# Every second band of two 3x3 convolutions formed from four mixtures of input rows (24 passes instead of 36)

## The chip, the cores and the metric

The kernel runs on one core of a Trainium2 chip. The metric is the time of one execution in microseconds (us). A core has five engines that run side by side, each with its own queue worked off in order: TensorE (PE in the profile; PEld is its loading of weights), VectorE (DVE), ScalarE (ACT), GpSimd (POOL) and SyncE (SP, which here only issues transfers). TensorE writes its sums to PSUM, a memory of 8 banks of 512 fp32 values per partition; everything else works on SBUF.

## What is computed

The input x is 4 images of 128 channels and 64 x 64 points, fp32. Two layers follow each other; cut to what matters:

```python
# layer 0: attention over the 4096 points of an image, 4 heads of 32 channels
x = x + proj(softmax(q @ k.T / sqrt(32)) @ v)      # q, k, v from the group-normed x
# layer 1: two convolutions with weights quantised to the integers -4..3 times alpha
def conv3x3(x, wq):                                # zero border of one point
    out = 0
    for kh in range(3):
        for kw in range(3):
            out = out + einsum('bchw,oc->bohw', xp[:, :, kh:kh+H, kw:kw+W], wq[:, :, kh, kw])
    return out
out = relu(batchnorm(conv3x3(x, wq1)))             # mean and variance over all images and points
out = relu(batchnorm(conv3x3(out, wq2)) + x)
```

A batch norm needs all results of its convolution before it can scale any of them.

## The kernel before, in words

**Attention first.** Most of the kernel is the attention (lines 425 to 769): scores (L442) and their weighting of v (L456) on TensorE, exponentials on ScalarE (L444), sums of exponentials on VectorE (L471). Its result y0 goes to DRAM, image by image. During its last blocks the first bands of the first convolution are already loaded and split.

**A band.** The convolutions work on 16 bands (`bandlist`), each 16 rows of one image (`BR`), 4 bands an image. A band's input tile has 18 rows of 66 points: the rows above and below and the border columns, which GpSimd sets to zero (`border`). TensorE multiplies here in a rounded form of fp32 (`F32R`). So the input is split (`split`): `hi` is the rounded input, a cast on VectorE (L573), and `lo` the rest, a subtraction (L574). `conv` makes one half of a band, 8 rows or 512 points, in one PSUM bank: for `hi` and then `lo`, nine taps each, a matmul (here "pass") of 512 columns against the 128 x 128 weights of that tap: 18 passes a half, 36 a band (L782). The weights are small integers, exact in the rounded form.

**A layer.** `layer(i, prepare, done)` goes through the bands. For each it queues the passes of the band; calls `prepare(m)`; then for each half queues statistics on VectorE (L848, read from PSUM) and a copy of the results to `cv` on ScalarE (L849). All queues keep this order: what `prepare(m)` gives to VectorE and ScalarE stands ahead of the statistics and copies of band m. Bands 0 and 1 of layer 0 are made before `layer` starts (`early`), between the last steps of the attention. The last band's halves have tiles of their own, and its statistics are merged with the others' at the end (L850 to L858). Then follow some idle matmuls (`keep_warm`) and `batch_norm`, which gives the scale and shift that the next stage needs.

**What prepare does.** In layer 0 it is `first(m)`: it issues the load of band m+3 (SP's queue) and splits band m+2. At m = 2 it loads the quantised weights of the second convolution from DRAM to `raw_w`, at m = 6 it casts them to `wq[1]`, at m = 5 `count_bad` counts values out of bounds, with a tiny matmul and a copy of its result on VectorE. In layer 1 it is `second(m)`: `relu_band` of band m+2 (a relu on ScalarE from `cv`, L891, then cast and subtraction on VectorE, L894 and L895), and the load of a part of y0 for the residual. The first input of layer 1 is made apart, in two pieces (L906 to L918).

**Buffers.** The input tiles `t`, `hi`, `lo` come from a pool of 9 (`kpool`, through `stack_tile`); a tile's place is used again when everything that read it is done. PSUM is `pss`, three tiles of two banks, one per ordinary band (`conv_tile`), and `psa`, two tiles of one bank, for the last band and small sums. The framework places all waits; on a PSUM tile, the operations of different engines are kept in the order in which they are written.

**The end.** After layer 1 the results are scaled, the residual is added (L948), the relu applied (L949) and the output stored.

Of the kernel before, what the change touches and what calls it, by code (L numbers as in the profile page):

```python
# [16 lines left out]
F32 = mybir.dt.float32  # L17
AF = mybir.ActivationFunctionType
ALU = mybir.AluOpType
# [3 lines left out]
P = 128  # L23
# [3 lines left out]
TAPS = 9  # L27
FB = 512
# [6 lines left out]
F32R = mybir.dt.float32r  # L35
# [43 lines left out]
def _fast_body(ctx, tc, x, norm_w, norm_b, qkv_wt, qkv_b, proj_wt, proj_b,  # L79
               w1, alpha1, gamma1, beta1, w2, alpha2, gamma2, beta2, out, cnt):  # L80
    nc = tc.nc
    B, C, H, W = x.shape
# [3 lines left out]
    NB = N // FB  # L86
# [3 lines left out]
    PW = W + 2  # L90
# [48 lines left out]
    wq = [const.tile([P, TAPS, P], F32R, name="wq0")]  # L139
    wqd = dram.tile([P, TAPS, P], F32, name="wqd")  # L140
# [68 lines left out]
    pss = ctx.enter_context(tc.tile_pool(name="pss", bufs=3, space=PSUM))  # L209
    psa = ctx.enter_context(tc.tile_pool(name="psa", bufs=2, space=PSUM))  # L210
    y0 = [dram.tile([P, N], F32, name=f"y0_{b}") for b in range(B)]
    BR = 2 * RB
# [11 lines left out]
    def stack_tile(name):  # L224
        return kpool.tile([P, KW], F32R, name=name, tag="k")

    def f32(t):
        return t.bitcast(F32)
# [326 lines left out]
    def band_tile(name):  # L555
        return stack_tile(name).rearrange("p (r w) -> p r w", w=PW)

    def border(t, g):

        nc.gpsimd.memset(f32(t)[:, :, 0:1], 0.0)  # L560
        nc.gpsimd.memset(f32(t)[:, :, W + 1 : W + 2], 0.0)
        r0, r1 = g * BR - 1, g * BR + BR + 1
        if r0 < 0:
            nc.gpsimd.memset(f32(t)[:, 0, 1 : 1 + W], 0.0)
        if r1 > H:
            nc.gpsimd.memset(f32(t)[:, BR + 1, 1 : 1 + W], 0.0)
        lo, hi = max(r0, 0), min(r1, H)
        return f32(t)[:, lo - r0 : hi - r0, 1 : 1 + W], lo, hi

    def split(t, name):  # L570

        hi, lo = band_tile(f"hi{name}"), band_tile(f"lo{name}")
        nc.vector.tensor_copy(hi, f32(t))  # L573
        nc.vector.tensor_tensor(lo, f32(t), f32(hi), ALU.subtract)  # L574
        return hi, lo

    raw, ready = {}, {}

    def load_band(b, g):
        raw[b, g] = t = band_tile(f"t0_{b}_{g}")  # L580
        inner, lo, hi = border(t, g)
        nc.sync.dma_start(out=inner, in_=y0[b].rearrange("p (h w) -> p h w", w=W)[:, lo:hi, :])

    def split_band(b, g):
        ready[0, b, g] = split(raw[b, g], f"0_{b}_{g}")


    halves = [ppool.tile([P, HEADS, FB], F32, name=f"xh{i}", tag="p") for i in range(2)]
# [6 lines left out]
    st = small.tile([P, NB, 6], F32, name="st0", tag="st")  # L595
# [144 lines left out]
    todo, parts = [], {}  # L740
# [29 lines left out]

    bandlist = [(b, g) for b in range(B) for g in range(H // BR)]

    def conv(parts, ps, j, w):
        hi, lo = parts
        r0 = j * RB
        n = 0
        for part in (hi, lo):
            for tap in range(TAPS):  # L780
                kh, kw = divmod(tap, 3)
                nc.tensor.matmul(ps.rearrange("p (r w) -> p r w", w=W), w[:, tap, :],  # L782
                                 part[:, r0 + kh : r0 + kh + RB, kw : kw + W],
                                 start=(n == 0), stop=(n == 2 * TAPS - 1))
                n += 1

    def conv_tile(i, b, g):
        return pss.tile([P, 2, FB], F32, name=f"c{i}_{b}_{g}", tag="s")
# [16 lines left out]

    mid = ctx.enter_context(tc.tile_pool(name="mid", bufs=1))
    cv = [mid.tile([P, N], F32, name=f"cv{b}") for b in range(B)]
    raw_w = mid.tile([P, TAPS, P], F32, name="raw_w")
    wq.append(mid.tile([P, TAPS, P], F32R, name="wq1"))


    a_q, a_g, a_n = ([small.tile([P, 1], F32, name=f"{n}{i}") for i in range(2)]
# [21 lines left out]
    def layer(i, prepare, done):  # L834


        st = mid.tile([P, B * NB, 6], F32, name=f"st{i}")
        end = mid.tile([P, 15], F32, name=f"end{i}")
        nc.gpsimd.memset(end[:, 0:1], float((B * NB - 2) * FB))
        for m, (b, g) in enumerate(bandlist[:-1]):  # L840
            ps = done[m] if m < len(done) else conv_tile(i, b, g)
            for j in range(2):
                if m >= len(done):
                    conv(ready[i, b, g], ps[:, j, :], j, wq[i])
            prepare(m)
            for j in range(2):
                c = 2 * g + j
                nc.vector.bn_stats(st[:, b * NB + c, :], ps[:, j, :])  # L848
                nc.scalar.copy(cv[b][:, c * FB : (c + 1) * FB], ps[:, j, :])  # L849
        nc.vector.bn_aggr(end[:, 1:3], st.rearrange("p j s -> p (j s)")[:, : 6 * B * NB - 12])  # L850
        nc.vector.tensor_scalar(end[:, 2:3], end[:, 2:3], float((B * NB - 2) * FB), None, ALU.mult)
        b, g = bandlist[-1]
        for j in range(2):
            ps = psa.tile([P, FB], F32, name=f"c{i}_last{j}", tag="a")
            conv(ready[i, b, g], ps, j, wq[i])
            c = 2 * g + j
            nc.vector.bn_stats(end[:, 3 + 6 * j : 9 + 6 * j], ps)
            nc.scalar.copy(cv[b][:, c * FB : (c + 1) * FB], ps)  # L858
        prepare(len(bandlist) - 1)
        keep_warm(10)  # L860
        return batch_norm(i, end)

    def count_bad():

        big = small.tile([P, 1], F32, name="big")
        nc.vector.tensor_reduce(big, worst, AX.X, ALU.max)
        bad = small.tile([P, 1], F32, name="bad")
        nc.vector.tensor_scalar(bad, big, LIMIT, None, ALU.is_gt)
        nbad = psa.tile([P, FB], F32, name="nbad", tag="a")
        nc.tensor.matmul(nbad[0:1, 0:1], bad, ones[:, 0:1], start=True, stop=True)  # L870
        nc.vector.tensor_copy(cnt, nbad[0:1, 0:1])

    def first(m):
        if m == 5:
            count_bad()
        if m == 2:
            nc.sync.dma_start(out=raw_w, in_=wqd)
        if m == 6:
            nc.vector.tensor_copy(wq[1], raw_w)
        if 0 < m < len(bandlist) - 3:  # L880
            load_band(*bandlist[m + 3])
        if m + 2 < len(bandlist) and m > 0:
            split_band(*bandlist[m + 2])

    a1, c1 = layer(0, first, early)

    def relu_rows(b, g, t, r0, r1):
# [8 lines left out]
                                f32(t["hi"])[:, r0:r1, :], ALU.subtract)  # L896

    def relu_band(b, g, pieces=((0, BR + 2),)):
        t = {n: band_tile(f"{n}1_{b}_{g}") for n in ("t", "hi", "lo")}
        t["inner"] = border(t["t"], g)  # L900
        for r0, r1 in pieces:
            relu_rows(b, g, t, r0, r1)
        ready[1, b, g] = t["hi"], t["lo"]


    b0, g0 = bandlist[0]  # L906
    t = {n: band_tile(f"{n}1_{b0}_{g0}") for n in ("t", "hi", "lo")}
    t["inner"] = border(t["t"], g0)
    hi_inner, lo_row, hi_row = border(t["hi"], g0)
    for r0, r1 in ((0, RB + 2), (RB + 2, BR + 2)):  # L910
        a, e = max(r0 + g0 * BR - 1, lo_row), min(r1 + g0 * BR - 1, hi_row)
        for dst in (hi_inner.bitcast(F32R), t["inner"][0]):
            nc.scalar.activation(dst[:, a - lo_row : e - lo_row, :],
                                 cv[b0].rearrange("p (h w) -> p h w", w=W)[:, a:e, :], AF.Relu,
                                 bias=c1, scale=a1)
# [26 lines left out]
    for b in range(B):  # L942
        for j in range(4):
            for p in range(2 if b == j == 0 else 1):
                n = HN // 2 if b == j == 0 else HN
                y = res[b, j][:, p * n : (p + 1) * n]
# [464 lines left out]
```

## Time and profile before

| what | us |
|---|---|
| median of 3 runs | 2547.48 (2546.02 to 2547.59) |
| the profiled execution | 2548.74 |
| its span, first to last instruction | 2547.0 |
| TensorE busy (share of the span) | 2509.0 (99%) |
| VectorE busy | 2137.2 (84%) |
| ScalarE busy | 2087.4 (82%) |
| passes of the convolutions, L782, one on average | 0.400 to 0.401 (pipelined: the next starts earlier) |
| first pass of layer 0 (band 0) starts at | 2234.0 |
| last statistics of layer 0 start at | 2375.32 |
| first pass of layer 1 starts at | 2378.84 |
| last statistics of layer 1 start at | 2516.48 |

Times inside the profile are counted from the first instruction of the span. A row of the groups gives line, engine, operation, output and inputs by the program's names, partitions x elements, how many, their busy time, the mean of one in ns, and the idle time of the engine just before them with what ended it. In the answers in order of time a row is one or several like instructions: start, length, engine, line; in brackets the idle time before it and what ended that. Matmuls overlap, so the cost of one is read from the distance of the starts, not from its length.

### The profile page before, as it was taken

The numbers are of one execution on the slowest core, as the hardware profiler recorded it, in microseconds if no ns is written. First come the engines' busy times: TensorE is split into PE (matmuls) and PEld (weight loads), VectorE is DVE, ScalarE is ACT, GpSimd is POOL, SyncE is SP. The second block draws the span as 40 slices with busy tenths as digits, with TensorE's granted clock in tenths as the row PEclk, the third lists the DMA queues.
The fourth block names the chain that finished last, engine by engine and source line by source line (L and its number), as shares of the span: only waits on it lengthen the run. The fifth ranks groups of instructions, "written<-read, shape, count | busy, mean of one in ns | idle before, by whom it ended". The sixth has DMA issues, their size and how long they took to land.

```text
span 2547.0 us, 65043 instructions
## 1 busy us (share of the span) xinstructions
PE 2509.0 (99%) x28708; PEld 1503.6 (59%) x28708; DVE 2137.2 (84%) x1402; ACT 2087.4 (82%) x2278; POOL 281.6 (11%) x461
## 2 busy tenths in 40 slices
PE   9999999999999999999999999999999999999995
PEld 6555555555555555555555555555555555577774
DVE  6899888889988889889988888889999999954445
ACT  5999888999988999999988899989999999911224
POOL 2111111111011111110111111111000011000000
PEclk9999999999999999999999999999999999999998
DMA  6877667788757667797766666796666666745004
GB/s 193 192 185 169 168 173 181 171 203 182 184 132 190 170 152 169 164 231 164 173 163 172 157 166 158 191 203 150 149 138 144 146 145 149 150 90 160 1 1 166
DMA packets 148954, 403.86 MB, mean 159 GB/s; under 512 B 59416, under 2 KB 60184, under 8 KB 120120
## 3 DMA queue, kind: packets, MB, share of 16 engines
q0 software_dynamic: 45840, 280.39, 48.2%
q1 hardware_dynamic: 100952, 113.60, 16.9%
q10 hardware_dynamic: 1872, 5.64, 0.6%
q8 instruction: 227, 3.72, 0.6%
q14 instruction: 63, 0.52, 0.1%
HBM read 107.48 MB, written 56.42 MB: 64 GB/s over the span
## 4 chain that ended last, share of the span: by engine, by line
PE 92%; issue 3%; DMA 2%; DVE 1%; ACT 1%; ACTq 0%; POOL 0%; SPq 0%; POOLq 0%; DVEq 0%
PE s L442 41%; PE acc L456 36%; PE c L782 9%; DMA rm<-p 2%; PE l L488 1%; PE pq L317 1%; PE pk L317 1%; PE po L317 1%; PE pv L317 1%; DVE r L471 1%; ACT p L444 0%; ACT res L949 0%; DMA xh<-in_x_dram 0%; PE c_last L782 0%; DVE res L948 0%
## 5 line engine op out<-in xcount | busy, mean ns | idle before, releaser
L444 ACT ACTIVATE p<-s 128x1024 f32<-128x1024 f32 x2048 | 1950.5, 1032 | 201.6 <-PE s L442 154.5
L471 DVE TENSOR_TENSOR r<-r,p 128x2048 f32<-128x2048 f32 x768 | 1758.2, 2289 | 65.0 <-ACT p L444 14.5
L442 PE MATMUL s<-q,k 64*128 64x512 f32 x8192 | 1138.6, 409 | 1.7 <-ACT p L444 0.9
L456 PE MATMUL acc<-p,v 128*32 128x256 f32 x16384 | 1026.4, 383 | 0.0
L442 PEld LDWEIGHTS s<-q,k 64*128 64x128 f32 x8192 | 715.4, 184 | 410.3 <-issue 165.3
L456 PEld LDWEIGHTS acc<-p,v 128*32 128x32 f32 x16384 | 462.4, 109 | 483.7 <-issue 248.5
L466 POOL DMA_DIRECT2D rm<-p x160 | 139.5, 872 | 800.4 <-ACT p L444 535.5
L849 ACT COPY cv<-c 128x512 f32<-128x512 f32 x60 | 35.2, 586 | 200.1 <-DVE st L848 200.1
L782 PE MATMUL c<-hi,wq 128*128 128x512 f32 x540 | 139.1, 401 | 1.3 <-issue 1.3
L782 PE MATMUL c<-lo,wq 128*128 128x512 f32 x540 | 138.5, 400 | 0.0
L848 DVE BATCH_NORM_STATS2 st<-c 128x6 f32<-128x512 f32 x60 | 41.9, 699 | 103.9 <-PE c L782 83.4
L782 PEld LDWEIGHTS c<-hi,wq 128*128 128x128 f32 x540 | 101.2, 188 | 30.3 <-issue 2.1
L782 PEld LDWEIGHTS c<-lo,wq 128*128 128x128 f32 x540 | 101.6, 188 | 27.2
L352 DVE SCALAR_TENSOR_TENSOR kst<-pk,b,kst 128x512 fp32r<-128x512 f32 x32 | 24.0, 751 | 83.6 <-PE s L442 68.5
L469 DVE TENSOR_TENSOR r<-p,p 128x2048 f32<-128x2048 f32 x32 | 73.2, 2288 | 12.1 <-ACT p L444 11.1
L352 DVE SCALAR_TENSOR_TENSOR qst<-pq,b,qst 128x512 fp32r<-128x512 f32 x32 | 24.0, 751 | 58.2 <-PE s L442 47.3
L356 POOL DMA_DIRECT2D qd<-qst x31 | 23.6, 760 | 262.7 <-DVE qst L352 220.8
L492 POOL DMA_DIRECT2D r<-rm x31 | 26.2, 844 | 220.4 <-DMA rm<-p 95.1
L356 POOL DMA_DIRECT2D kd<-kst x27 | 20.0, 740 | 175.8 <-DVE kst L352 167.2
L488 PE MATMUL l<-r,ones 128*32 128x256 f32 (+1 forms) x504 | 37.7, 382 | 0.0
L464 POOL DMA_DIRECT2D rm<-p x32 | 17.8, 557 | 176.8 <-ACT p L444 93.4
L351 ACT ACTIVATE kst<-pk,b 128x512 fp32r<-128x512 f32 x32 | 22.3, 699 | 18.2 <-PE pk L317 18.2
(149 smaller groups left out, 739.3 us busy)
## 6 DMA issues: line engine op xcount, KB each, us to landing
rm<-p POOLq DMA_DIRECT2D x192, 1024.0 KB, 7.9
q<-qd SPq DMA_DIRECT2D x248, 128.0 KB
r<-rm POOLq DMA_DIRECT2D x31, 1024.0 KB, 7.6
x<-in_x_dram SPq DMA_DIRECT2D x86, 256.0 KB
k<-kd SPq DMA_DIRECT2D x124, 128.0 KB
qd<-qst POOLq DMA_DIRECT2D x31, 512.0 KB, 5.3
kd<-kst POOLq DMA_DIRECT2D x27, 512.0 KB, 4.8
y<-x POOLq DMA_DIRECT2D x32, 256.0 KB, 6.2
```

Source lines behind the costliest of these rows:

```text
L317: nc.tensor.matmul(out[cs, :], w[:, cs], x, start=True, stop=True)
L352: nc.vector.scalar_tensor_tensor(lo, ps[what], bias, t[:, 0, :], ALU.add, ALU.subtract)
L356: (nc.sync if start else nc.gpsimd).dma_start(out=dst[b, j].rearrange("s p n -> p s n"), in_=t)
L442: nc.tensor.matmul(s[:, i, :], k[r, half, c0 : c0 + P], q[r, half, part, :], start=(part == 0), stop=(part == 1))
L444: nc.scalar.activation(pts[step][:, 2 * half : 2 * half + 2, :], s, AF.Exp, scale=SCALE)
L456: nc.tensor.matmul(acc[n][h * D : (h + 1) * D, cs], v[:, kt % KB, h * D : (h + 1) * D], pt[:, h, cs], start=(kt == 0 and half == 0), stop= ...
L466: nc.gpsimd.dma_start(out=msum[n], in_=pt, accum_op=ALU.add)
L469: nc.vector.tensor_tensor(rsum[n], pts[step - 1], pt, ALU.add)
L471: nc.vector.tensor_tensor(rsum[n], rsum[n], pt, ALU.add)
L488: nc.tensor.matmul(t["l"][h * D : (h + 1) * D, cs], ones, r[:, h, cs], start=first, stop=end)
L782: nc.tensor.matmul(ps.rearrange("p (r w) -> p r w", w=W), w[:, tap, :], part[:, r0 + kh : r0 + kh + RB, kw : kw + W], start=(n == 0), stop ...
L848: nc.vector.bn_stats(st[:, b * NB + c, :], ps[:, j, :])
```

## The change

With rows d0 to d3 of the input and the three rows of weights g0, g1, g2, two neighbouring rows of results are

- m0 = (d0 - d2) g0, m1 = (d1 + d2) (g0 + g1 + g2)/2, m2 = (d2 - d1) (g0 - g1 + g2)/2, m3 = (d1 - d3) g2
- upper row: m0 + m1 + m2; lower row: m1 - m2 - m3

Each product is a convolution along the row alone, with 3 taps. For the 16 rows of a band each product has 8 rows, 512 points: 3 taps for `hi` and 3 for `lo`, 6 passes, and four products, 24 passes. Bands 3, 5, 7, 9, 11, 13 of layer 0 and 2, 4, 6, 8, 10, 12, 14 of layer 1 (`BY_TWO`) are made in this way; the others as before.

- `mixed` takes the place of `split` there: on VectorE the differences (`outer`, 16 rows) and the two halves of `inner` (8 rows each), on ScalarE the two rounded copies, on VectorE the two rests. Three of its tiles come from `kpool` (as does the input), three from a new pool of 6 (`upper`).
- `mix_weights` makes (g0+g1+g2)/2 and (g0-g1+g2)/2 on VectorE, for layer 0 ahead of the layer, for layer 1 at band 14.
- `conv_by_two` forms m1 and m2 in a tile of `pss`, then m0 and m3 in a second tile of `pss` or, every second time, in the two tiles of `psa`.
- `rows_of_two` combines them: a copy on ScalarE and four operations on VectorE, straight into `cv`. The statistics then read `cv` in SBUF; the two copies to `cv` fall away.
- The weights of the second convolution are loaded to a tile of `kpool` at band 5 instead of to `raw_w` at band 2; `count_bad` comes at band 4 instead of 5.

```diff
--- before.py
+++ after.py
@@ -575,6 +575,35 @@
         return hi, lo
 
     raw, ready = {}, {}
+    bandlist = [(b, g) for b in range(B) for g in range(H // BR)]
+
+
+
+
+    BY_TWO = (set((3, 5, 7, 9, 11, 13)), set((2, 4, 6, 8, 10, 12, 14)))
+
+    def mixed(t, name):
+
+
+        t = f32(t)
+        outer, inner = (stack_tile(f"{n}{name}")[:, : BR * PW].rearrange("p (r w) -> p r w", w=PW)
+                        for n in ("vo", "vi"))
+        nc.vector.tensor_tensor(f32(outer), t[:, 0:BR, :], t[:, 2 : BR + 2, :], ALU.subtract)
+        odd, even = t[:, 1 : BR + 1 : 2, :], t[:, 2 : BR + 2 : 2, :]
+        nc.vector.tensor_tensor(f32(inner)[:, : BR // 2, :], odd, even, ALU.add)
+        nc.vector.tensor_tensor(f32(inner)[:, BR // 2 :, :], even, odd, ALU.subtract)
+        def part(n):
+            if n == "uo":
+                return stack_tile(f"{n}{name}")[:, : BR * PW].rearrange("p (r w) -> p r w", w=PW)
+            return upper.tile([P, BR, PW], F32R, name=f"{n}{name}", tag="u")
+
+        hi, lo = ([part(n + k) for k in "oi"] for n in "ul")
+        for u, v in zip(hi, (outer, inner)):
+            nc.scalar.copy(u, f32(v))
+        for u, v, w in zip(hi, (outer, inner), lo):
+            nc.vector.tensor_tensor(w, f32(v), f32(u), ALU.subtract)
+        return [(o[:, 0::2, :], i[:, : BR // 2, :], i[:, BR // 2 :, :], o[:, 1::2, :])
+                for o, i in (hi, lo)]
 
     def load_band(b, g):
         raw[b, g] = t = band_tile(f"t0_{b}_{g}")
@@ -582,7 +611,8 @@
         nc.sync.dma_start(out=inner, in_=y0[b].rearrange("p (h w) -> p h w", w=W)[:, lo:hi, :])
 
     def split_band(b, g):
-        ready[0, b, g] = split(raw[b, g], f"0_{b}_{g}")
+        way = mixed if bandlist.index((b, g)) in BY_TWO[0] else split
+        ready[0, b, g] = way(raw[b, g], f"0_{b}_{g}")
 
 
     halves = [ppool.tile([P, HEADS, FB], F32, name=f"xh{i}", tag="p") for i in range(2)]
@@ -770,8 +800,6 @@
 
 
 
-    bandlist = [(b, g) for b in range(B) for g in range(H // BR)]
-
     def conv(parts, ps, j, w):
         hi, lo = parts
         r0 = j * RB
@@ -805,8 +833,41 @@
 
     mid = ctx.enter_context(tc.tile_pool(name="mid", bufs=1))
     cv = [mid.tile([P, N], F32, name=f"cv{b}") for b in range(B)]
-    raw_w = mid.tile([P, TAPS, P], F32, name="raw_w")
     wq.append(mid.tile([P, TAPS, P], F32R, name="wq1"))
+    upper = ctx.enter_context(tc.tile_pool(name="upper", bufs=6))
+    wmix = mid.tile([P, 2, 3, P], F32R, name="wmix")
+
+    def mix_weights(i):
+
+        g0, g1, g2 = (f32(wq[i])[:, 3 * k : 3 * k + 3, :] for k in range(3))
+        h = f32(stack_tile(f"wsum{i}"))[:, : 3 * P].rearrange("p (t o) -> p t o", o=P)
+        nc.vector.tensor_tensor(h, g0, g2, ALU.add)
+        nc.vector.tensor_scalar(h, h, 0.5, None, ALU.mult)
+        for k, f in enumerate((0.5, -0.5)):
+            nc.vector.scalar_tensor_tensor(wmix[:, k, :, :], g1, f, h, ALU.mult, ALU.add)
+
+    def conv_by_two(parts, a, c, i):
+
+        for m, ps, w in ((1, a[0], wmix[:, 0, :, :]), (2, a[1], wmix[:, 1, :, :]),
+                         (0, c[0], wq[i][:, 0:3, :]), (3, c[1], wq[i][:, 6:9, :])):
+            n = 0
+            for part in parts:
+                for kw in range(3):
+                    nc.tensor.matmul(ps.rearrange("p (r w) -> p r w", w=W), w[:, kw, :],
+                                     part[m][:, :, kw : kw + W], start=(n == 0), stop=(n == 5))
+                    n += 1
+
+    def rows_of_two(a, c, y):
+
+        even, odd = (y.rearrange("p (r e w) -> p r e w", e=2, w=W)[:, :, e, :] for e in range(2))
+        a0, a1, c0, c1 = (u.rearrange("p (r w) -> p r w", w=W) for u in (*a, *c))
+        nc.scalar.copy(odd, a1)
+        nc.vector.tensor_tensor(even, odd, a0, ALU.add)
+        nc.vector.tensor_tensor(odd, a0, odd, ALU.subtract)
+        nc.vector.tensor_tensor(even, even, c0, ALU.add)
+        nc.vector.tensor_tensor(odd, odd, c1, ALU.subtract)
+
+    mix_weights(0)
 
 
     a_q, a_g, a_n = ([small.tile([P, 1], F32, name=f"{n}{i}") for i in range(2)]
@@ -838,6 +899,21 @@
         end = mid.tile([P, 15], F32, name=f"end{i}")
         nc.gpsimd.memset(end[:, 0:1], float((B * NB - 2) * FB))
         for m, (b, g) in enumerate(bandlist[:-1]):
+            if m in BY_TWO[i]:
+                a = conv_tile(i, b, g)
+                a = [a[:, j, :] for j in range(2)]
+                if sorted(BY_TWO[i]).index(m) % 2:
+                    c = [psa.tile([P, FB], F32, name=f"c{i}_{b}_{g}{j}", tag="a") for j in "xy"]
+                else:
+                    c = pss.tile([P, 2, FB], F32, name=f"c{i}_{b}_{g}z", tag="s")
+                    c = [c[:, j, :] for j in range(2)]
+                conv_by_two(ready[i, b, g], a, c, i)
+                prepare(m)
+                y = cv[b][:, 2 * g * FB : (2 * g + 2) * FB]
+                rows_of_two(a, c, y)
+                for j in range(2):
+                    nc.vector.bn_stats(st[:, b * NB + 2 * g + j, :], y[:, j * FB : (j + 1) * FB])
+                continue
             ps = done[m] if m < len(done) else conv_tile(i, b, g)
             for j in range(2):
                 if m >= len(done):
@@ -871,12 +947,15 @@
         nc.vector.tensor_copy(cnt, nbad[0:1, 0:1])
 
     def first(m):
+        if m == 4:
+            count_bad()
         if m == 5:
-            count_bad()
-        if m == 2:
-            nc.sync.dma_start(out=raw_w, in_=wqd)
+            raw["w"] = f32(stack_tile("raw_w"))[:, : TAPS * P].rearrange("p (t o) -> p t o", o=P)
+            nc.sync.dma_start(out=raw["w"], in_=wqd)
         if m == 6:
-            nc.vector.tensor_copy(wq[1], raw_w)
+            nc.vector.tensor_copy(wq[1], raw["w"])
+        if m == 14:
+            mix_weights(1)
         if 0 < m < len(bandlist) - 3:
             load_band(*bandlist[m + 3])
         if m + 2 < len(bandlist) and m > 0:
@@ -896,6 +975,13 @@
                                 f32(t["hi"])[:, r0:r1, :], ALU.subtract)
 
     def relu_band(b, g, pieces=((0, BR + 2),)):
+        if bandlist.index((b, g)) in BY_TWO[1]:
+            t = band_tile(f"t1_{b}_{g}")
+            inner, lo, hi = border(t, g)
+            nc.scalar.activation(inner, cv[b].rearrange("p (h w) -> p h w", w=W)[:, lo:hi, :],
+                                 AF.Relu, bias=c1, scale=a1)
+            ready[1, b, g] = mixed(t, f"1_{b}_{g}")
+            return
         t = {n: band_tile(f"{n}1_{b}_{g}") for n in ("t", "hi", "lo")}
         t["inner"] = border(t["t"], g)
         for r0, r1 in pieces:
```

## The prediction

> **What bounds the kernel now.** I read the slices first, then the chain, the groups of the two convolution layers, and last the queues in order of time. The table of engines, the slices and the chain of work that ended last:
>
> ```profile
> PE 2509.0 (99%) x28708; PEld 1503.6 (59%) x28708; DVE 2137.2 (84%) x1402; ACT 2087.4 (82%) x2278; POOL 281.6 (11%) x461
> ...
> DVE  6899888889988889889988888889999999954445
> PE 92%; issue 3%; DMA 2%; DVE 1%; ACT 1%; ACTq 0%; POOL 0%; SPq 0%; POOLq 0%; DVEq 0%
> PE s L442 41%; PE acc L456 36%; PE c L782 9%; DMA rm<-p 2%; PE l L488 1%; PE pq L317 1%; PE pk L317 1%; PE po L317 1%; PE pv L317 1%; DVE r L471 1%; ACT p L444 0%; ACT res L949 0%; DMA xh<-in_x_dram 0%; PE c_last L782 0%; DVE res L948 0%
> ```
>
> TensorE ends last everywhere, in the convolutions (L782, the last 310 us) too. There VectorE's last slices fall to 4 to 5 tenths: half of it is free for what the change adds. TensorE in order of time, four bands of layer 0, and the stretches of one band in each layer (columns: length, then busy us and counts of PE, PEld, DVE, ACT, POOL):
>
> ```profile
> 2254.51 34.54 PE c L782 x144
> ...
> 2263.10:2271.70 8.60, 8.60 (x37) 6.79 (x36) 6.15 (x7) 2.31 (x4) 0.24 (x3) 1.00 0.83 150
> 2421.80:2430.40 8.60, 8.60 (x37) 6.78 (x36) 3.58 (x4) 2.38 (x3) 0.18 (x2) 1.00 0.00 0
> ```
>
> A band of 36 passes takes 8.60 us, so a pass takes 8.60/36 = 0.239 us, at full clock and with no gap. VectorE in order of time, where layer 0 begins and in the middle of layer 1:
>
> ```profile
> 2256.74 0.16 DVE L517 TENSOR_TENSOR worst<-worst,most 128x1 f32<-128x1 f32 x1
> ...
> 2258.16 0.70 DVE L848 BATCH_NORM_STATS2 st<-c 128x6 f32<-128x512 f32 x1 [0.60 <-DMA y<-x]
> 2259.55 0.70 DVE L848 BATCH_NORM_STATS2 st<-c 128x6 f32<-128x512 f32 x1 [0.70 <-ACT cv L849]
> 2260.17 0.76 DVE L573 CAST hi<-t 128x1188 fp32r<-128x1188 f32 x1
> 2260.96 1.40 DVE L574 TENSOR_TENSOR lo<-t,hi 128x1188 fp32r<-128x1188 f32 x1
> ...
> 2422.03 0.70 DVE L848 BATCH_NORM_STATS2 st<-c 128x6 f32<-128x512 f32 x1 [2.34 <-PE c L782]
> 2423.44 0.70 DVE L848 BATCH_NORM_STATS2 st<-c 128x6 f32<-128x512 f32 x1 [0.71 <-ACT cv L849]
> 2426.07 0.78 DVE L894 CAST hi<-t 128x1188 fp32r<-128x1188 f32 x1 [1.93 <-ACT t L891]
> ```
>
> At the start of layer 0 VectorE is late: band 3's split ends at 2262.4, and TensorE takes band 3 at 2263.1. In layer 1 each new input waits 1.9 us: the relu stands on ScalarE behind the second copy of the band before. The statistics start only when both halves of a band are done.
>
> **What the Trainium skill says.** "VectorE: DVE Perf Modes", section "The TRN2 errata", prices an fp32 two-source operation at (N+151)/0.96 ns. The trace agrees: 1.397 us for 1188 elements. "ScalarE: Activation LUTs", section "What ACT_TABLE_LOAD costs", gives 186 ns + 0.833 N without pointer operands; the copy of 512 from PSUM took 586 ns against 613. "TensorE: Matmul & The Clock Gate", section "Wait — 56ns, not 53.3ns?", has 216 ns for 512 columns; here it is 239, and that counts. "PSUM — Partial Sum Buffer", section "Terms", forbids two engines on one bank at a time; this trace shows copy, statistics, copy strictly in turn, and I let the new operations take turns too.
>
> **The change, part by part.**
>
> *TensorE.* A mixed band makes four products of 6 passes, each again 512 columns against 128x128 weights. I take 0.239 us a pass: only the distance between the rows read is new. Bounds: 0.216 (the skill's figure) and 0.36, where 24 passes cost what 36 do. Saved: 12 x 0.239 = 2.87 us a band, over 6 + 7 = 13 bands **37.3 us**. A mixed band lasts 5.73 us, a pair of bands 14.33 instead of 17.2.
>
> *VectorE.* Durations are from rows where there is one; neighbours without a dependence overlap by about 0.07 us (2260.96 + 1.40 ends after the next start, 2262.28). Removed per mixed band: cast 0.77, subtraction 1.40, two PSUM statistics. Added:
> - inputs: three operations of 1056 elements at (1056+151)/0.96 = 1.26 us and two of 528 at 0.71: 5.2 less overlaps, 5.0. ScalarE's two rounding copies, 186 + 0.833 x 1056 = 1.07 us each, run beside the next operations; bare they would add about 1 us a band.
> - rows of results: four operations of 512 with one PSUM input; the bias addition to v (L371), the same kind, has 0.684 us: 2.56 with overlaps. Bounds 0.60 and 1.1, since rows every second place are not in the trace. The copy that precedes them (0.59) is ScalarE's, made while TensorE still forms the other two products.
> - statistics from SBUF, 2 x 0.686 (L688): 1.25 net, with no copies between.
>
> Sum 8.8 us. An ordinary band keeps 2.1 for its split and 1.96 for statistics with the copy between (2280.50 to 2282.46). A pair needs 12.9 us in layer 0, below 14.33. In layer 1 the wait of 1.9 us for the relu stays before each mixed input (the ordinary band before still has copies), but goes before the ordinary one, because a mixed band leaves ScalarE no copy after its statistics. That is 14.8 us: VectorE falls 0.5 to 0.6 us further behind with each pair.
>
> *Start of layer 0.* `mix_weights(0)` is put on VectorE in front of the first statistics: an addition and a scaling of 384 (0.56 and 0.36) and two scaled additions (0.61, as L186), 2.1 us; the last must also wait for the landing that held the statistics until 2258.16. Band 0's statistics start at about 2259.9 and end at 2261.9; band 3's mixed input ends at 2266.9. The first three passes of band 3 need only the rounded parts, so it starts at 2266.2 where TensorE was free at 2263.1: **3.1 us** lost. Its second pair of sums takes the PSUM of band 1, whose statistics are queued behind the mixed input and whose last copy ends at 2269.6, while TensorE wants it at 2266.2 + 2.87: **0.5**. Band 4 then takes band 2's tile, free at 2273.8, wanted at 2272.5: **1.3**. So 4.9, and 0.1 for small waits. Afterwards VectorE recovers: 2.3 us late at band 4, 1.4 at band 6, on time from band 8. Moving the count of bad values one band earlier costs nothing visible: its matmul waits less than 0.1 us for VectorE; VectorE waits about 0.6 for the matmul.
>
> *Layer 1.* VectorE is on time at band 1, 0.6 us late at band 3, about 3.6 at band 13. Who waits: after a mixed band with two tiles of the pool of three, the next ordinary band takes the tile of the ordinary band before it. It has the mixed band's 5.73 us less 2.7 for statistics and copies, some 3.0 us of grace. The lateness there is 1.2 (band 7 after 5) and 2.4 (11 after 9): covered. The inputs' lead over TensorE shrinks from 5 us (band 4) to 2 us (band 14): covered, just. Band 15 is ordinary and its sums lie in the pool of single banks, so the end finds VectorE caught up. I count 0.2.
>
> *Moved or hidden.* The load of the second layer's weights goes three bands later on SP's queue, ahead of the load of band 8, which is needed 30 us later; its cast at band 6 still precedes layer 1 by 60 us. `mix_weights(1)`, 2.1 us, falls in the 5 us in which VectorE awaits band 14. POOL's border memsets stay. Of the nine input tiles at most four are held when a mixed band takes three more, so these come from bands already convolved; the six of the new pool hold two mixed bands. Uncovered, each of these would cost its own length once, under 3 us.
>
> *Sum.* 37.3 - 5.0 - 0.2 = 32.1. Following the queues of the unchanged kernel with the same durations gives its layers within 0.3 us. I take 2 us off for signals between engines that no row shows: a gain of **30 us**. The profiled execution took 2548.74 us, of which the span was 2547.0; 2518.7 after. The median shown is 1.26 us lower: **2517.5 us**.
>
> **Rivals.**
> 1. *VectorE becomes the bound.* The nine added operations cost more than their kind, through strided rows or signals. For: layer 1 has no room. Against: the formula fits every fp32 row. With 1 us more per mixed band the gain falls to 26 us, with 2 us to 16: 2522 to 2532. Chance 0.15.
> 2. *The same loop past break-even, slower.* Place: the four results operations, between PSUM's release and the next statistics. Layer 1's pair would have to pass 17.2 us instead of 14.8, layer 0's also: with 3.4 us more per mixed band, that is about 1.55 us instead of 0.684 per operation, the gain is gone; with 4 us the kernel is 7 us slower, 2554. Against: only the rows' spacing is new, runs of 64 remain. Chance 0.07.
> 3. *Passes get dearer.* Rows read two apart for two of the products, or new weights not hidden behind the pass (a load takes 188 ns of 239). At 0.28 us a pass 20 us are left, 2527. Chance 0.07. Below that the pass is as it was.
> 4. *Nothing happens*, because what is saved is waited for elsewhere: 2547. The unbroken TensorE rows speak against it. Chance 0.03.
>
> The likeliest case has 0.68; its own range is 2512 (stall at the start halved) to 2523. The range reaches over most of rivals 1 and 3: 2511 to 2530. A difference under 0.2% (5 us) can't be told from none. Faster: 0.68 + 0.14 + 0.07 = 0.89; same: 0.01 + 0.03 = 0.04; slower 0.07.
>
> **What would show it.** Right: mixed bands of 24 passes in 5.7 us; one hole of TensorE of about 3 us at band 3, then 0.5 and 1.3, waiting for VectorE and for the copies; none in layer 1; results operations near 0.69 us, big mixtures near 1.26. Layer 0 shorter by 12, layer 1 by 20. Also possible: the trace grants a clock of 0.56 to the last 27 us, in which TensorE is idle; a hole of 3 us may lower it too, which the row of clocks would show, and I allow up to 2 us for it. Wrong: holes at every pair (rival 1 or 2), passes over 0.25 us (rival 3), or input tiles that wait for a convolution still running.

## The result and the profile after

The changed kernel takes **2516.0 us** (median of 4 runs, 2515.08 to 2520.64) against 2547.53 before (median of 4), a ratio of **0.988** with a 95% interval of 0.9865 to 0.9895: 31.5 us faster. Its profiled execution took 2515.98 us, of which the span was 2514.1.

The page of the changed kernel: the table of engines, VectorE's slices and the chain of work that ended last:

```profile
PE 2472.6 (98%) x28552; PEld 1474.0 (59%) x28552; DVE 2205.4 (88%) x1501; ACT 2106.9 (84%) x2291; POOL 283.1 (11%) x461
...
DVE  6899888899988988889988889879999999978687
...
PE 87%; DMA 4%; issue 4%; DVE 3%; ACT 1%; SPq 1%; ACTq 0%; POOL 0%; POOLq 0%; DVEq 0%
```

TensorE has 36.4 us less work, VectorE 68 us more, and VectorE's slices in the convolutions rise from 4 to 5 tenths to 6 to 8 (the last five). To place the gain, I measure a layer from the start of its first pass to the start of its last statistics, in each profile:

| | before | after | difference |
|---|---|---|---|
| start of the span to layer 0's first pass | 2233.99 | 2232.93 | -1.1 |
| layer 0 | 141.33 | 129.81 | -11.5 |
| to layer 1's first pass | 3.52 | 3.55 | 0.0 |
| layer 1 | 137.64 | 117.77 | -19.9 |
| from there to the end of the span | 30.5 | 30.0 | -0.5 |

The two layers gave 31.4 us. The first row is the attention, which the change leaves alone; the convolutions start between 2230.2 and 2234.2 us in the profiles of this study.

The groups of the new operations, convolution stretch only (columns as in the page):

```profile
L915 DVE BATCH_NORM_STATS2 st<-cv 128x6 f32<-128x512 f32 x26 | 16.7, 685 | 0.4
L604 DVE TENSOR_TENSOR li<-vi,ui 128x1056 fp32r<-128x1056 f32 x13 | 16.4, 1259 | 0.0
L591 DVE TENSOR_TENSOR vo<-t 128x1056 f32<-128x1056 f32 x13 | 16.3, 1251 | 11.7 <-ACT t L981 11.7
L602 ACT CAST ui<-vi 128x1056 fp32r<-128x1056 f32 x13 | 14.0, 1078 | 2.1 <-DVE vi L594 2.0
L866 DVE TENSOR_TENSOR cv<-c,cv 128x512 f32<-128x512 f32 x13 | 9.0, 691 | 0.5
L865 DVE TENSOR_TENSOR cv<-cv,c 128x512 f32<-128x512 f32 x13 | 8.9, 681 | 1.1 <-ACT cv L864 1.1
```

Rows that lie two apart cost nothing extra: the large mixtures take 1.25 us, the operations on the results 0.68 to 0.69.

The start of layer 0, TensorE in order of time (start, length; in brackets the idle time before and what ended it):

```profile
2259.91 2.31 PE L810 MATMUL c<-lo,wq 128*128 128x512 f32 x9
2265.20 1.65 PE L856 MATMUL c<-ui,wmix 128*128 128x512 f32 x3 [2.98 <-ACT ui L602]
2266.64 1.49 PE L856 MATMUL c<-li,wmix 128*128 128x512 f32 x3
2267.94 0.98 PE L856 MATMUL c<-ui,wmix 128*128 128x512 f32 x3
...
2273.21 2.42 PE L810 MATMUL c<-hi,wq 128*128 128x512 f32 x9 [0.72 <-ACT cv L925]
```

and VectorE in order of time:

```profile
2257.92 1.03 DVE L847 SCALAR_TENSOR_TENSOR wmix<-wq,wsum 128x384 fp32r<-128x384 f32 x2 [1.21 <-DMA y<-x]
...
2259.51 0.69 DVE L924 BATCH_NORM_STATS2 st<-c 128x6 f32<-128x512 f32 x1
2260.90 0.70 DVE L924 BATCH_NORM_STATS2 st<-c 128x6 f32<-128x512 f32 x1 [0.70 <-ACT cv L925]
2261.51 1.24 DVE L591 TENSOR_TENSOR vo<-t 128x1056 f32<-128x1056 f32 x1
...
2265.18 1.26 DVE L604 TENSOR_TENSOR li<-vi,ui 128x1056 fp32r<-128x1056 f32 x1
2266.35 0.69 DVE L924 BATCH_NORM_STATS2 st<-c 128x6 f32<-128x512 f32 x1
```

TensorE is free at 2262.06 (2259.91 and nine passes) and waits for band 3's mixed input; I call this wait the hole. The first six passes after the hole take 2.74 us instead of 1.43: the granted clock is lower, as the stretches show (columns: length, busy us and counts of PE, PEld, DVE, ACT, POOL, then the granted clock, the DMA's share and GB/s):

```profile
2262.00:2265.20 3.20, 0.23 (x2) 0.01 (x1) 3.20 (x5) 2.36 (x3) 0.17 (x2) 0.93 0.58 133
2265.20:2268.70 3.50, 3.50 (x9) 2.65 (x10) 2.85 (x5) 0.86 (x2) 0.00 (x0) 0.58 0.29 52
2268.70:2272.50 3.80, 3.79 (x16) 2.63 (x15) 3.04 (x5) 0.90 (x2) 0.24 (x3) 1.00 0.14 33
```

Band 4 starts at 2273.21; without any loss it would be 2262.06 + 5.73 = 2267.79. The start loses **5.4 us**. The chain that the profile follows back from band 4 runs over the copies and statistics of bands 2 and 1, the mixing of band 3's input, the statistics of band 0 and the mixing of the weights (L847), to the landing of an output of the attention (`y<-x`), behind which the last part of the weights' mixing starts at 2257.92: VectorE's queue sets the start of band 4. The whole of layer 0 loses 5.7 against its full saving (141.33 - 6 x 2.87 = 124.11), layer 1 only 0.2 (137.64 - 7 x 2.87 = 117.55).

Layer 1, VectorE in order of time, the statistics of two ordinary bands and what lies between:

```profile
2413.28 0.69 DVE L924 BATCH_NORM_STATS2 st<-c 128x6 f32<-128x512 f32 x1
2414.63 0.70 DVE L924 BATCH_NORM_STATS2 st<-c 128x6 f32<-128x512 f32 x1 [0.65 <-ACT cv L925]
2417.25 1.26 DVE L591 TENSOR_TENSOR vo<-t 128x1056 f32<-128x1056 f32 x1 [1.92 <-ACT t L981]
...
2428.01 0.69 DVE L924 BATCH_NORM_STATS2 st<-c 128x6 f32<-128x512 f32 x1
```

VectorE's pair of bands takes 2428.01 - 2413.28 = 14.73 us, 1.92 of it waiting for the relu; TensorE's takes 14.32. Once layer 1 has begun, TensorE has no gap in it.

### The profile page after: what moved, and what is told of

It reads as the page before. It is cut to its first block, busy times and chain, and to the rows that moved or that the text cites. A ratio compares the mean times of both kernels' runs of the same rounds, so it can differ in the third digit from the quotient of the medians.

```text
span 2514.1 us, 64863 instructions
## 1 busy us (share of the span) xinstructions
PE 2472.6 (98%) x28552; PEld 1474.0 (59%) x28552; DVE 2205.4 (88%) x1501; ACT 2106.9 (84%) x2291; POOL 283.1 (11%) x461
## 4 chain that ended last, share of the span: by engine, by line
PE 87%; DMA 4%; issue 4%; DVE 3%; ACT 1%; SPq 1%; ACTq 0%; POOL 0%; POOLq 0%; DVEq 0%
PE s L442 40%; PE acc L456 36%; PE c L810 4%; DMA rm<-p 2%; DVE r L471 1%; DMA rc<-rd 1%; PE l L488 1%; PE pk L317 1%; PE pq L317 1%; PE c L856 1%; PE pv L317 1%; PE po L317 1%; DMA q<-qd 1%; SPq L422 0%; PE c_2z L856 0%
## 5 line engine op out<-in xcount | busy, mean ns | idle before, releaser
L925 ACT COPY cv<-c 128x512 f32<-128x512 f32 x34 | 20.0, 587 | 130.3 <-DVE st L924 130.3
L469 DVE TENSOR_TENSOR r<-p,p 128x2048 f32<-128x2048 f32 x32 | 73.2, 2288 | 11.1 <-ACT p L444 11.0
L810 PE MATMUL c<-hi,wq 128*128 128x512 f32 x306 | 79.1, 402 | 2.1 <-ACT hi L999 1.4
L810 PE MATMUL c<-lo,wq 128*128 128x512 f32 x306 | 78.5, 400 | 0.0
L810 PEld LDWEIGHTS c<-hi,wq 128*128 128x128 f32 x306 | 57.2, 188 | 19.7 <-issue 3.6
L810 PEld LDWEIGHTS c<-lo,wq 128*128 128x128 f32 x306 | 57.6, 188 | 15.4
L356 POOL DMA_DIRECT2D qd<-qst x31 | 23.6, 762 | 267.0 <-DVE qst L352 223.0
L924 DVE BATCH_NORM_STATS2 st<-c 128x6 f32<-128x512 f32 x34 | 23.7, 696 | 20.0 <-ACT cv L925 11.2
```

What stands on the lines that cost most here:

```text
L356: (nc.sync if start else nc.gpsimd).dma_start(out=dst[b, j].rearrange("s p n -> p s n"), in_=t)
L469: nc.vector.tensor_tensor(rsum[n], pts[step - 1], pt, ALU.add)
```

## The experiments

Theory A: each pass saved is worth 0.239 us, and the only price is VectorE's lateness at the start of layer 0; everywhere else its new work hides. Rivals: the layers depend on each other's backlog (B); the mixing of the weights makes the hole (C); part of the gain comes from something other than passes (D); the lowered clock is the cost (E); VectorE is late at band 4 anyhow, and a wait for the count of bad values only hides it (F); VectorE's growing lateness in layer 1 costs something (G). All layer times are read as in the table above.

| kernel | median us | ratio to before, 95% interval | layer 0 | layer 1 |
|---|---|---|---|---|
| layer0_only | 2537.0 | 0.9954 (0.9937 to 0.9971) | 130.21 | 137.67 |
| layer1_only | 2528.06 | 0.9919 (0.9903 to 0.9936) | 141.40 | 117.72 |
| passes_36 | 2552.64 | 1.0021 (1.0014 to 1.0028) | 146.36 | 137.76 |
| skip_band3 | 2514.25 | 0.9865 (0.985 to 0.988) | 126.99 | 117.70 |
| warm_hole | 2515.27 | 0.9875 (0.9858 to 0.9891) | 129.76 | 117.75 |
| vector_plus1 | 2523.78 | 0.9904 (0.9887 to 0.992) | 131.89 | 124.92 |
| vector_plus2 | 2537.57 | 0.9965 (0.9955 to 0.9975) | 137.23 | about 131.8 |
| relu_early | 2516.17 | 0.9871 (0.9856 to 0.9886) | 130.15 | 117.76 |
| relu_plus1 | 2518.06 | 0.988 (0.9865 to 0.9895) | 132.13 | 117.76 |
| later_start | 2513.76 | 0.9865 (0.9849 to 0.9882) | 126.56 | 117.74 |
| later_count | 2511.37 | 0.9858 (0.9842 to 0.9875) | 124.24 | 117.76 |
| later_count_relu | 2510.46 | 0.9849 (0.9835 to 0.9862) | 124.24 | 117.75 |

The kernel before, run beside them on the same chip, had medians of 2547.29 us (beside layer0_only, layer1_only, passes_36 and later_start), 2547.37 (warm_hole, vector_plus1, vector_plus2 and later_count) and 2548.5 (the other four).

### One layer at a time

```diff
-    BY_TWO = (set((3, 5, 7, 9, 11, 13)), set((2, 4, 6, 8, 10, 12, 14)))
+    BY_TWO = (set((3, 5, 7, 9, 11, 13)), set())      # layer0_only; no mix_weights(1)
+    BY_TWO = (set(), set((2, 4, 6, 8, 10, 12, 14)))  # layer1_only; no mix_weights(0)
```

> Mixed bands in layer 0 only; layer 1 as in the kernel before. Theory A (every pass saved is worth 0.239 us, and the only cost is the late VectorE at the start of layer 0, 5.5 us): layer 0 is 11.5 us shorter from its first pass to its last statistics (6 x 2.87 - 5.5 = 11.7), layer 1 keeps its 137.6 us, the whole gains 11 to 12 us on the kernel before. Rival B (VectorE's work is what limits both layers, and the two layers share its backlog): more or less than the part that the changed kernel shows, by over 2 us.

> Mixed bands in layer 1 only, and no mixing of the first layer's weights. Theory A: layer 0 keeps its 141.3 us, layer 1 needs 117.8 us, gain 19.9 us (7 x 2.87 = 20.1). Rival B: layer 1 is longer or shorter than in the changed kernel by over 1 us, since VectorE enters it differently.

Layer 0 alone gains 11.1 us in the profile and 10.3 in the medians, layer 1 alone 19.9 and 19.2. Each layer is as long as in the changed kernel within 0.4 us, and the other as before within 0.1. The layers add up; B falls.

### All the work of the change, but 36 passes

```diff
-            for part in parts:
+            for part in (parts[0], parts[0], parts[1]):
                 for kw in range(3):
                     nc.tensor.matmul(ps.rearrange("p (r w) -> p r w", w=W), w[:, kw, :],
-                                     part[m][:, :, kw : kw + W], start=(n == 0), stop=(n == 5))
+                                     part[m][:, :, kw : kw + W], start=(n in (0, 3)), stop=(n in (2, 8)))
```

Three passes of each product are made and thrown away (the next one starts the sum anew).

> The changed kernel with three extra passes for each product, which are made and thrown away: mixed bands have 36 passes again, and everything else of the change stays. Theory A: all 37.3 us of the gain go, the start of layer 0 still loses 3 to 5.5 us, so 2 to 5 us above the kernel before, 2550 to 2553. Rival D (part of the gain comes from elsewhere: the copies that fall away, statistics read from SBUF, fewer waits on PSUM): below the kernel before, 2545 or less.

Layer 1 is back at 137.76 us, 0.1 from before: all of its gain is passes, and all its other work is hidden or free (behind 36 passes here; that it hides behind 24 as well is seen in the changed kernel, whose layer 1 loses only 0.2 us). Layer 0 is 5.0 us longer than before: that is the price at the start, bare. TensorE in order of time there (band 3's first and band 4's first passes):

```profile
2265.39 2.43 PE L856 MATMUL c<-ui,wmix 128*128 128x512 f32 x6 [3.13 <-ACT ui L602]
...
2275.60 2.31 PE L810 MATMUL c<-hi,wq 128*128 128x512 f32 x9
```

The hole is 3.1 us, the lowered clock costs some 1.6 us more (10.21 us for band 3's passes, where 36 x 0.239 is 8.60), and band 4, later here, waits for nothing. D falls.

### What makes the hole

```diff
-    BY_TWO = (set((3, 5, 7, 9, 11, 13)), set((2, 4, 6, 8, 10, 12, 14)))
+    BY_TWO = (set((5, 7, 9, 11, 13)), set((2, 4, 6, 8, 10, 12, 14)))   # skip_band3
```

> The changed kernel with band 3 of layer 0 made as before (36 passes, split); the weights are still mixed ahead of the layer. Theory A (band 3's mixed input, ahead of the statistics of band 1, is most of the loss at the start; the mixing of weights alone delays band 3's split by about 2 us past its need): TensorE waits some 1.5 us before band 3 and is otherwise unbroken, layer 0 = 129.8 + 2.87 - (5.5 - 1.5) = 128.7 us, a gain with one mixed band less. Rival C (the mixing of the weights makes the hole): the loss of 5.5 us stays, layer 0 132.7 us.

Layer 0 takes 126.99 us, which is 141.33 - 5 x 2.87 = 126.98: with one mixed band less it is 2.8 us shorter, and nothing is lost at all. The mixing of the weights alone makes no hole, and C falls as it was put; the 1.5 us that I had expected it to cost were wrong. It is still a part of the hole in the changed kernel: there the statistics of band 0 start 1.59 us after the landing (2257.92 to 2259.51), with the last two operations of the mixing and six small ones between, and all that follows on VectorE is that much later. In the kernel before, the small ones were done ahead of the landing, and the statistics started right behind it. Without the mixing the hole would be some 1.4 us (an estimate, 2.98 - 1.59); no run takes it away and keeps band 3 mixed. VectorE and TensorE in order of time in this kernel:

```profile
2260.23 0.76 DVE L573 CAST hi<-t 128x1188 fp32r<-128x1188 f32 x1
2261.03 1.40 DVE L574 TENSOR_TENSOR lo<-t,hi 128x1188 fp32r<-128x1188 f32 x1
```

```profile
2261.58 2.31 PE L810 MATMUL c<-hi,wq 128*128 128x512 f32 x9
2263.73 2.31 PE L810 MATMUL c<-lo,wq 128*128 128x512 f32 x9
```

An ordinary band's first nine passes read only the rounded part, ready at 2261.0; the rest is needed 2.15 us later. A mixed band has three such passes, 0.7 us, before it needs its last rest. The mixed input is worse placed here by its length (4.9 against 2.1 us) and by its order of use. The landing matters too: counted from the layer's first pass it came at 24.99 us in the changed kernel and at 25.31 in relu_early, whose hole was 3.3 us instead of 3.0; in skip_band3 it came at 24.18. So some tenths of a microsecond in layer 0 are chance.

### The lowered clock

```diff
+                if i == 0 and m == 3:
+                    keep_warm(11)
                 conv_by_two(ready[i, b, g], a, c, i)
```

> The changed kernel with 22 idle matmuls of 128 columns (2.6 us of them) put in front of band 3's passes in layer 0, where TensorE waits 3.0 us and then works band 3 at a lowered clock, about 1.4 us longer. Theory A (band 4 can't start before band 2's tile is free, whatever band 3 does): band 3 runs at the full clock, the waits for PSUM in it and after it come back, layer 0 stays at 129.8 us within 0.4. Rival E (the lowered clock is itself the cost): layer 0 is 1 to 1.4 us shorter.

Idle matmuls now fill most of the hole. Layer 0 takes 129.76 us, 0.05 from the changed kernel. TensorE in order of time:

```profile
2263.82 0.98 PE L856 MATMUL c<-ui,wmix 128*128 128x512 f32 x3 [0.48 <-ACT ui L602]
2265.11 0.98 PE L856 MATMUL c<-li,wmix 128*128 128x512 f32 x3 [0.32 <-DVE li L604]
...
2267.69 0.98 PE L856 MATMUL c_3z<-uo,wq 128*128 128x512 f32 x3 [0.18 <-ACT cv L927]
...
2271.83 2.43 PE L810 MATMUL c<-hi,wq 128*128 128x512 f32 x9 [1.01 <-ACT cv L927]
```

Band 3 runs at full clock (1.00 granted from 2262.0 to 2272.5), and now the waits for PSUM that were predicted inside band 3 (0.2) and ahead of band 4 (1.0) appear. Band 4's start is set by VectorE, through band 2's statistics and copies; the lowered clock only fills that time. E falls.

### How much room VectorE has

```diff
         nc.vector.tensor_tensor(f32(outer), t[:, 0:BR, :], t[:, 2 : BR + 2, :], ALU.subtract)
+        for _ in range(1):     # vector_plus1; 2 in vector_plus2
+            nc.vector.tensor_tensor(f32(outer), t[:, 0:BR, :], t[:, 2 : BR + 2, :], ALU.subtract)
```

> Each mixed input makes its large difference twice, 1.19 us more of VectorE per mixed band. Theory A (VectorE's pair takes 12.9 and 14.8 us against TensorE's 14.3, so layer 0 has 1.4 us to spare and layer 1 nothing): layer 0 about 2 us longer than in the changed kernel (all at its start), layer 1 about 5 to 6 us longer, since the lateness grows by 1.6 us a pair and meets the reuse of PSUM at 3 us; in all 2523 to 2525. Rival (VectorE is hidden throughout): no change, within 1 us of 2516.

> The large difference made three times, 2.38 us more of VectorE per mixed band. Theory A: VectorE sets the pace in both layers, 15.3 and 17.2 us a pair; layer 0 about 7 us and layer 1 about 14 us longer than in the changed kernel, 2535 to 2539, nearly the time of the kernel before. Rival (the gain falls in proportion, no threshold): half of what vector_plus1 loses twice over, so the loss of this run is twice that of vector_plus1.

With 1.19 us more per mixed band layer 0 grows by 2.1 us and layer 1 by 7.2; with 2.38 us by 7.4 and 14.0. Of a gain of 31.5 us, 23.6 and 9.8 are left. The loss is not in proportion (7.9 and 21.7 us). It is layer 0 that bends (2.1 and 7.4): it has a threshold in between. Layer 1 loses in proportion from the first addition on (7.2 and 14.0): it stands at its threshold already. TensorE in layer 1 of vector_plus1, all rows with idle time but the first of the layer, and the two rows behind the second:

```profile
2419.97 2.41 PE L812 MATMUL c<-hi,wq 128*128 128x512 f32 x9 [0.75 <-ACT cv L927]
...
2452.07 4.21 PE L812 MATMUL c<-hi,wq 128*128 128x512 f32 x9 [2.90 <-ACT cv L927]
2456.08 3.29 PE L812 MATMUL c<-lo,wq 128*128 128x512 f32 x9
2459.21 2.31 PE L812 MATMUL c<-hi,wq 128*128 128x512 f32 x9
```

These are bands 7 and 11, each behind a mixed band that holds two of the three large PSUM tiles, waiting for the copies of bands 5 and 9. Behind a hole of 2.9 us the passes are slow again, and for longer: eighteen take 7.14 us from start to start, where 4.30 are due. No later wait was there to swallow these 2.8 us; layer 1 lost 1 to 2 us more than I had expected, and they are in it.

### The wait for the relu in layer 1

```diff
-        if m + 2 < len(bandlist):
-            relu_band(*bandlist[m + 2])
+        if m + 3 < len(bandlist):
+            relu_first(*bandlist[m + 3])    # border and relu (ScalarE), one band earlier
+        if m + 2 < len(bandlist):
+            relu_rest(*bandlist[m + 2])     # mixed or split (VectorE)
```

> In layer 1 the relu of band m+3 is put on ScalarE where that of band m+2 stood, one band earlier, so that VectorE does not wait 1.9 us for it before a mixed input. Theory A (VectorE's growing lateness in layer 1 meets nobody): layer 1 stays at 117.7 us within 0.3, with VectorE's pair bound to TensorE's 14.33 us instead of 14.75. Rival G (the lateness costs something at the end or in the tile reuse): layer 1 shorter by 0.5 us or more.

> relu_early with the large difference made twice, as in vector_plus1, whose layer 1 was 7.2 us longer than the changed kernel's. Theory A (the wait for the relu is what leaves layer 1 without room): VectorE's pair is about 12.9 + 1.2 + 0.5 = 14.6 us, so layer 1 is at most 1 us longer than 117.7; layer 0 is as in vector_plus1, 131.9. Rival (VectorE's own work is the bound there): layer 1 stays near 125.

Taken away alone, the wait changes nothing: layer 1 117.76 us. G falls. With the extra 1.19 us on VectorE, the same edit brings layer 1 from 124.92 down to 117.76. VectorE in order of time in relu_plus1:

```profile
2400.66 0.70 DVE L926 BATCH_NORM_STATS2 st<-c 128x6 f32<-128x512 f32 x1 [0.65 <-ACT cv L927]
2401.27 1.24 DVE L591 TENSOR_TENSOR vo<-t 128x1056 f32<-128x1056 f32 x1
...
2413.65 0.70 DVE L926 BATCH_NORM_STATS2 st<-c 128x6 f32<-128x512 f32 x1 [0.24 <-PE c L812]
```

The mixed input starts with no wait, and before the next statistics VectorE is idle again, 0.24 us, waiting for TensorE. So it was the wait behind ScalarE that took layer 1's room: without it VectorE has 1.19 us and a little more to spare in each pair.

### A version that beats both

```diff
-    BY_TWO = (set((3, 5, 7, 9, 11, 13)), set((2, 4, 6, 8, 10, 12, 14)))
+    BY_TWO = (set((4, 6, 8, 10, 12, 14)), set((2, 4, 6, 8, 10, 12, 14)))
...
-    mix_weights(0)
...
-                if sorted(BY_TWO[i]).index(m) % 2:
+                if (sorted(BY_TWO[i]).index(m) + (i == 0)) % 2:
...
     def first(m):
-        if m == 4:
+        if m == 3:
             count_bad()
+        if m == 2:
+            mix_weights(0)
```

> Layer 0's mixed bands are 4, 6, ..., 14 instead of 3, 5, ..., 13; its weights are mixed at band 2 instead of ahead of the layer; the count of bad values comes at band 3, and layer 0's mixed bands begin with the single-bank tiles. Theory A: no hole at the start, layer 0 about 124 to 126 us (141.3 - 17.2, up to 2 us left over), the whole 3.5 to 5.5 us below the changed kernel, 2510.5 to 2512.5. Rival B: the backlog moves with the bands, and layer 0 stays within 1.5 us of 129.8.

Layer 0 takes 126.56 us, a little beyond the range I had expected and 2.5 more than the full saving of 17.2 us leaves (124.1). TensorE in order of time:

```profile
2267.11 2.32 PE L810 MATMUL c<-lo,wq 128*128 128x512 f32 x9
2271.06 0.19 PE L945 MATMUL nbad<-ones,bad 128*1 128x1 f32 x2 [1.63 <-DVE bad L943]
2271.85 0.95 PE L856 MATMUL c<-ui,wmix 128*128 128x512 f32 x3 [0.60 <-ACT cv L924]
```

The tiny matmul that counts bad values stands in TensorE's queue and waits for VectorE. So its three steps were taken apart:

```diff
-        if m == 3:
-            count_bad()
+        for part, at_m in enumerate((3, 5, 6)):   # VectorE's part, the matmul, VectorE's copy
+            if m == at_m:
+                count_bad(part)
```

> later_start with the count of bad values in three places: VectorE's part at band 3, the tiny matmul at band 5, its copy at band 6, since the matmul at band 3 held TensorE 1.6 us for VectorE and 0.6 us were lost after it. Theory A: layer 0 124.1 to 124.8 us (141.3 - 17.2), the whole 2.4 us below later_start, 5 to 6 us below the changed kernel. Rival F (VectorE is late at band 4 anyhow, the matmul only hid it): layer 0 stays at 126 us or more.

Layer 0 takes 124.24 us. Of all TensorE's waits from layer 0 on, one is left, at the start of layer 1 (answer: engine, line, what it waited for, us, times, longest):

```profile
PE c L810 <- ACT hi L1006: 1.3, 1, 1.3
```

F falls. The hole is gone with the mixed bands beginning one band later and the weights mixed behind the first statistics; these two moves were made together, and which of them is worth how much is not shown. With relu_early added:

> later_count and relu_early together. Theory A: no more than later_count, layer 0 124.2 and layer 1 117.7 us, 2510 to 2512. Rival G: up to 1 us faster.

No difference that the intervals could tell: 2510.46 against 2511.37 us, both layers equal within 0.01. The thirteen mixed bands now give 37.0 of the 37.3 us of their passes in the two layers; the medians are 36 and 38 us below the kernel before.

## Why the prediction was right

Predicted were 2517.5 us and a range of 2511 to 2530; measured 2516.0. The mechanism was as predicted: TensorE is the bound, VectorE's new work hides behind it, and the one loss lies at the start of layer 0. Rival 4 fell with the result. Some of the parts were not as predicted:

- *A pass is worth 0.239 us.* Right. A mixed band takes 5.75 us (2296.57 to 2302.32; predicted 5.73), and passes_36 gives the whole gain of layer 1 back, 19.99 of 19.87 us. Rival 3 is out.
- *VectorE's 8.8 us per mixed band.* Measured 8.64 (from 2272.45 to 2281.09). The operations on inputs and results lay at the price of their kind, which is also what the Trainium skill gives ("VectorE: DVE Perf Modes", section "The TRN2 errata", (N + 151) / 0.96 ns: by estimate 1257 ns for 1056 elements, measured 1251 to 1259); rivals 1 and 2 fall with it. That the formula fits every fp32 row was said too widely: the scaled additions with one scalar per partition lie above it (L186, 384 elements, 619 ns, where an estimate by it is 557). The two for the weights have a constant instead and took 554 each, less than the 610 taken from L186. The rivals' slope was near: for 1 and 2 us more I had gains of 26 and 16; measured with 1.19 and 2.38 us more, 23.6 and 9.8.
- *Layer 1: 14.8 us a pair, lateness 0.5 to 0.6 a pair, 3.6 at band 13, covered.* A pair takes 14.73. The lateness did not follow from my own figures: 14.8 - 14.33 is 0.47 a pair, 2.8 in six; measured are 0.41 a pair. At band 13 the statistics start at 2472.28; the next pass starts at 2469.55 and statistics on time follow 0.2 later, so VectorE was 2.5 us late: less than predicted, and covered. So the inputs' lead over TensorE shrank from 5.3 us (band 4) to 3.1 (band 14), not to 2. The place where it would have met TensorE, bands 7 and 11, is shown by vector_plus1.
- *Start of layer 0: 3.1 + 0.5 + 1.3.* The sum, 5.0 with small waits, was near: 5.4 measured to the start of band 4, 5.7 in the whole layer. Its parts were not all there. The hole was 3.0. The lowered clock, which I had only as a possibility, took some 1.3 us in the first six passes, and it swallowed the 0.5 and part of the 1.3 (0.72 left). warm_hole shows that the sum does not depend on it, since VectorE sets the start of band 4; but the prediction did not say that this loss would fall into a wait, and behind the hole of vector_plus1 it did not. That was luck. The weights' mixing is part of the delay, as predicted, but only ahead of a mixed band 3: skip_band3 loses nothing with it in place.
- *Copy and statistics in turn.* The two halves of an ordinary band lie in two banks of one tile, and yet the second half's statistics wait for the first half's copy. The turns are thus the framework's order on the tile; they say nothing of the rule on single banks beside which the prediction put them.
- *Moving the count of bad values costs nothing.* Right as put: TensorE did not wait, VectorE waited 0.77 us. One band earlier still, it cost 1.6 us (later_start).
- *Two us taken off for signals that no row shows.* Not needed. The sum gave 32.1, and the layers gave 31.4. Without this reserve the prediction would have been 2515.5; the reserve, not the mechanism, is the distance between 2517.5 and 2516.0.

Not settled: how far beyond every second band one could go. In the last version VectorE waits about 1 us for TensorE in each pair; a further mixed band adds some 4.5 us to VectorE (8.64 less the 4.1 of an ordinary band) and takes 2.87 from TensorE. It was not tried. Nor was another order of the four products in band 3, or of its input's operations: the rounded `outer` is ready at 2263.91, the rounded `inner`, with which the passes begin, at 2265.14.

## What to carry to other kernels

Work moved from a bound engine to another one is free until one period of that other engine, with its waits for third engines, passes the bound engine's period; beyond that, only as long as the lateness that adds up stays under the grace that the buffers give (here 0.41 us a pair, against some 3 us in all by the prediction's estimate). Write down both periods, and take out a wait before taking out work. The first use of a new scheme needs its longer preparation at the moment when the pipeline has no lead: here the loss was gone when it began one band later, its weights were mixed later too, and the count no longer stood in the way. A tiny instruction in the bound engine's queue that waits for the other one costs what that engine is late.

## What the runs showed of the hardware

- Behind a hole of 3.0 us in TensorE's work the granted clock was 0.58 on average over 3.5 us, and six passes took 2.74 instead of 1.43 us. With the hole cut to 0.48 us (warm_hole) it was 1.00 and the passes ran at full speed. Holes of like length had different prices: band 3's 24 passes took 1.4 us more behind 3.0 us, its 36 passes 1.6 more behind 3.1 (passes_36), eighteen passes 2.8 more behind 2.9 (vector_plus1). Why they differ is not shown.
- VectorE reads PSUM as well as SBUF. Its additions and subtractions of two fp32 inputs took no longer with rows two apart or with one input from PSUM: 512 elements 0.68 to 0.69 us in all forms seen, with both inputs from SBUF 0.686 (L537 before).
- Reading statistics of 512 elements from SBUF instead of PSUM saves only 0.013 us (0.686, L688 before, against 0.699); what is saved is the wait for the copy between them: up to the start of the next operation, two from SBUF take 1.20 us (2279.89 to 2281.09) and two from PSUM 1.96 (2280.50 to 2282.46 before).
